# Edge search of a graph layer: one-hots with the chunk outside and rows in a run, and twelve tiles' means and variances by ScalarE

## The chip, the cores and the metric

The kernel runs on one core of a Trainium2 chip. A core has five engines that work side by side and meet at semaphores: TensorE (PE in the profile, with its weight loads shown apart as PEld), VectorE (DVE), ScalarE (ACT), GpSimd (POOL) and SyncE (SP, which here only issues transfers). Each engine works through its own instructions in the order in which they were issued. The metric is the device time of one execution in microseconds, and the time of a kernel is the median of its runs.

## The reference

The kernel computes two layers, each a graph part followed by a mixture of experts, on 3125 nodes with 256 features and 50000 edges. The change concerns only the start of the first graph part. Cut to what matters:

```python
edge_index = jnp.stack([src, dst])
x = x + _L0_gnn_ref(_layernorm(x, axis=-1), edge_index, L0_gnn_W, L0_gnn_b)
x = x + _L0_ffn_ref(_layernorm(x, axis=-1)[None], ...)[0]
x = x + _L1_gnn_ref(_layernorm(x, axis=-1), ..., src, dst)
x = x + _L1_ffn_ref(_layernorm(x, axis=-1)[None], ...)[0]

def _L0_gnn_ref(x, edge_index, W, b):
    dst, src = (edge_index[0], edge_index[1])
    agg = jnp.zeros_like(x).at[dst].set(x[src])
    h = jnp.concatenate((x, agg), axis=-1)
    return h @ W.T + b
```

Here `edge_index[0]`, the array `src` of the inputs, is the node that receives. Each node takes the normalised row of one neighbour: that of the last edge in the list that names it as receiver. The kernel therefore has to find, for every node, the last edge that points to it.

## The kernel before

**Tiling.** The nodes are T = 25 tiles of 128 rows (the last has 53), held in `X`. The 50000 edges are CD = 391 chunks of 128 edges, one edge to each partition. NG = 13 groups of GE = 31 chunks make up the search; GP is 32, one more than GE.

**The search.** Of a receiver's number, `qi` is the place in its tile (0 to 127) and `ri` the tile (0 to 24). For a group `g`, `one_hots(g)` on VectorE makes three things in bf16: `hot`, which holds a one where an edge's place is met (128 values for each of the group's chunks), `tiles[:, 0]`, the same for the tile number (25 values), and `tiles[:, 1]`, that one-hot times a power of two that grows with the chunk (`wb`). In the kernel before the chunk is the innermost index of all three (`[P, P, GP]` and `[P, 2, T, GP]`), and the table that the numbers are compared with, `spread`, is laid out in the same way. TensorE then takes, for every chunk, `hot[:, :, j]` as weights and `tiles[:, :, :, j]` as the 50 moving columns and adds up the group in one bank of PSUM (`sa` for even groups, `sb` for odd ones): the sums hold, for every node, how many edges it receives and, in the exponent, the last chunk of the group that has one. ScalarE copies them to `sums`. After the last group VectorE works out from `sums` the last chunk of every node (`expo`, `key`, `last`, ..., `chunk`). GpSimd gathers that chunk's edges (`er`, from the table `etab`), VectorE picks the edge and its sender (`pick`, `pmax`, `nbr`), and GpSimd gathers the sender's row (`near`, from the table `ztab`).

**What runs beside it.** The loop over the 13 groups also carries the normalisation. `stat(X[:, t, :], mvx, t)` takes a tile's mean and variance on VectorE (`bn_stats`, `bn_aggr`), `root` the root of the variance on ScalarE, `scales` the reciprocal and the shift `minus` on VectorE; `norm_x` normalises a tile on ScalarE (`xn`), `plus_bias` adds the bias to `X` on GpSimd, `turn_x` transposes the normalised tile on TensorE and copies it to `hT` on ScalarE, and `times_w` multiplies it by the weights, copies the product to `zs` on ScalarE and stores it in `ztab`. `edge_rows` writes `etab`, and `gate_products` works on the gates' weights in the first iterations. Transfers of zeros into later tables (`clears`) and of the edges (`wrows`, `wtab`) are issued by SP in the same loop.

**Order.** The order of the instructions on every engine is that of the program (a manual schedule of all five). One iteration `g` issues: `one_hots(g + 2)`, two groups ahead of the matmuls and into one of three buffers; the statistics of tile `g`; at even `g` the scales of the two tiles before; the matmuls of group `g`; `root`; the copy to `sums`; `edge_rows`; then `turn_x` for tile g - 3 and `times_w` for tile g - 4, and at even `g` `norm_x` and `plus_bias` for the tiles g - 2 and g - 1. The remaining twelve tiles have their statistics in the last two iterations (`late`): 13 to 18 at g = 11, and 19 to 24 at g = 12. After the loop come the last two `scales`, the search's end from `expo` on, and `norm_x`, `turn_x` and `times_w` for the remaining tiles.

**Other one-hots in the kernel.** `count_edges` (lines 1212 to 1233) and `list_steps` (lines 794 to 805, with the matmuls of line 788) make one-hots with the chunk outside: the number is held twice side by side, and two helpers lay both operands out in pairs of neighbours:

```python
def pairs(ap, n):
    return ap[:, :, None, :].to_broadcast([P, ap.shape[1], n // 2, 2])
def in_pairs(ap):
    return ap.rearrange("p m (n i) -> p m n i", i=2)
```

Lines that the text names: 376, 378 and 380 (the one-hots), 427 (the search's weights and matmuls), 431 (`sums`), 263 and 264 (`stat`), 267 (`root`), 270 and 271 (`scales`), 274 (`xn`), 312 and 313 (`turn_x`), 320 and 323 (`times_w`), 326 (`ztab`), 338 (`plus_bias`), 449 (`expo`), 502 (`er`), 508 to 515 (picking the edge), 519 (`near`), 1013 (the experts' first matmul), 1489 (a Square with an accumulated sum, in the second layer).

## Time and profile before

| | us |
|---|---|
| median of 3 runs (1099.32 to 1104.02) | 1102.59 |
| the profiled execution | 1105.5 |
| its span, from the first to the last instruction | 1103.7 |
| PE busy in it | 1001.9 (91%) |
| DVE busy | 603.2 (55%) |
| ACT busy | 325.2 (29%) |
| POOL busy | 339.7 (31%) |
| the 391 search matmuls, first and last start | 10.3 and 72.2 |

The busy time of an engine is the time in which at least one of its instructions was under way; a matmul counts until its end, and matmuls overlap, so a busy PE need not be at its peak. The mean granted clock of TensorE was 0.945 of full speed. The search is over in the first 75 us of the span; the experts of the first layer start at about 159 us. In views of the trace, a line gives the start of an instruction or of several alike in us, their length together, the engine, the line of the kernel, what was written from what, the shape and the number; in square brackets stands how long the engine had been idle before, and what ended that.

### The profile page before, as it was taken

The page shows a single profiled execution, that of the slowest core. Times are in us where ns is not written, and L with a number is a line of the kernel's source. Part 1 is how long each engine was busy: PE and PEld are TensorE (multiplying, and loading weights), DVE is VectorE, ACT ScalarE, POOL GpSimd, SP SyncE. Part 2 cuts the span into 40 slices and gives each one's busy share as a digit, 9 for nine tenths or more (in the row PEclk, how much of TensorE's full clock was granted, in tenths as well). Part 3 has the DMA queues.
Part 4 walks back from the last instruction along what each step waited for, and adds up shares of the span by engine and source line. Part 5 has one row for each costly group of instructions (what it writes and reads, how often), then busy time and mean ns, then how long its engine had stood idle before and what let it go on. Part 6 is the DMA issues. An engine that isn't in the chain of part 4 may idle for free. (4 is left out here: it accounts for less than half of the span.)

```text
span 1103.7 us, 16184 instructions
## 1 busy us (share of the span) xinstructions
PE 1001.9 (91%) x6057; PEld 755.0 (68%) x6057; DVE 603.2 (55%) x1571; ACT 325.2 (29%) x712; POOL 339.7 (31%) x357
## 2 busy tenths in 40 slices
PE   6998569998999999999998889999999999998990
PEld 6986436664667667777766668877877878665670
DVE  9975873772645556665544144354157253486563
ACT  1353411221335566666422112121011111312110
POOL 1236445422433112222322111011012235365450
PEclk9979779998999999999999989999989999898995
DMA  7665464532368767776552080411113112764875
GB/s 215 218 174 167 133 215 128 166 128 87 121 207 282 262 229 282 272 253 227 189 174 75 23 330 6 159 81 60 64 57 117 50 48 82 235 216 155 275 260 175
DMA packets 121073, 182.09 MB, mean 165 GB/s; under 512 B 20370, under 2 KB 97143, under 8 KB 120864
## 3 DMA queue, kind: packets, MB, share of 16 engines
q1 hardware_dynamic: 98947, 123.68, 34.7%
q0 software_dynamic: 13200, 34.14, 9.4%
q10 hardware_dynamic: 8836, 23.13, 5.5%
q8 instruction: 50, 0.82, 0.3%
q14 instruction: 40, 0.32, 0.1%
HBM read 108.30 MB, written 74.64 MB: 166 GB/s over the span
## 5 line engine op out<-in xcount | busy, mean ns | idle before, releaser
L1013 PE MATMUL big<-xs,w 128*128 128x512 f32 (+1 forms) x640 | 283.6, 566 | 7.2 <-ACT hid L1017 7.1
L1026 PE MATMUL y<-w,hid 128*128 128x256 f32 x1120 | 270.8, 387 | 6.8 <-DVE y L1031 5.4
L1026 PEld LDWEIGHTS y<-w,hid 128*128 128x128 f32 x1120 | 203.9, 191 | 33.6 <-DVE y L1031 8.1
L1667 PEld LDWEIGHTS <-at 128*128 128x128 bf16 x1875 | 186.7, 100 | 35.7 <-DMA at<-atab 9.2
L1035 POOL DMA_INDIRECT ytab<-y,put x112 | 123.5, 1102 | 206.8 <-DVE y L1031 146.9
L1017 ACT ACTIVATE hid<-big,bt 128x512 f32<-128x512 f32 (+1 forms) x160 | 101.3, 634 | 231.7 <-PE big L1013 208.4
L1013 PEld LDWEIGHTS big<-xs,w 128*128 128x128 f32 x640 | 112.8, 194 | 72.7 <-issue 36.6
L1667 PE MATMUL big<-parts,at 128*128 128x256 bf16 x1200 | 152.9, 282 | 8.2 <-DMA at<-atab 8.2
L1031 DVE TENSOR_TENSOR y<-y,b2t 128x256 f32<-128x256 f32 x112 | 47.2, 423 | 110.1 <-PE y L1026 109.3
L970 POOL DMA_INDIRECT g<-xtab,take x56 | 56.9, 1016 | 154.3 <-PE tr L987 115.9
L1232 PEld LDWEIGHTS <-hq 128*128 128x128 bf16 x800 | 57.2, 98 | 61.0 <-issue 40.4
L1212 DVE TENSOR_TENSOR hq<-qs,iota_b 128x2048 bf16<-128x2048 bf16 x50 | 61.1, 1222 | 54.2 <-PE sb L1232 54.2
L1667 PE MATMUL sa<-parts,at 128*128 128x256 bf16 x525 | 63.6, 273 | 0.0
L988 DVE COPY xs<-tr 128x512 f32<-128x512 f32 (+1 forms) x64 | 37.1, 618 | 48.3 <-PE tr L987 48.3
L1233 ACT CAST at<-sa 128x400 bf16<-128x400 f32 x100 | 49.1, 491 | 47.7 <-PE sa L1232 45.1
L1076 DVE SCALAR_TENSOR_TENSOR X<-y,weight,X 128x256 f32<-128x256 f32 (+1 forms) x78 | 37.7, 506 | 42.4 <-DMA y<-ytab 41.4
L1477 ACT COPY hT<-tr 128x512 f32<-128x512 f32 x25 | 14.4, 586 | 152.5 <-PE tr L1475 152.5
L1233 ACT CAST at<-sb 128x400 bf16<-128x400 f32 x100 | 49.0, 490 | 31.6 <-PE sb L1232 30.1
L1504 POOL TENSOR_TENSOR X<-X,kept 128x256 f32<-128x256 f32 x14 | 10.4, 770 | 129.7 <-DVE kept L496 129.7
L1215 DVE TENSOR_TENSOR hc<-cs,iota_b 128x1600 bf16<-128x1600 bf16 x50 | 49.2, 985 | 0.0
L1469 DVE SCALAR_TENSOR_TENSOR both<-big,deg,feat 128x256 f32<-128x256 f32 x16 | 7.7, 480 | 70.3 <-PE big L1667 70.2
L427 PEld LDWEIGHTS <-hot 128*128 128x128 bf16 x391 | 40.4, 150 | 6.6 <-issue 3.6
(349 smaller groups left out, 1244.0 us busy)
## 6 DMA issues: line engine op xcount, KB each, us to landing
w<-in_fW SPq DMA_DIRECT2D x32, 1024.0 KB
atab<-at ACTq DMA_DIRECT2D x25, 800.0 KB
at<-atab SPq DMA_DIRECT2D x25, 800.0 KB
ytab<-zero_b SPq DMA_DIRECT2D x10, 1024.0 KB
y<-ytab SPq DMA_DIRECT2D x19, 512.0 KB
w<-in_mw SPq DMA_DIRECT2D x32, 256.0 KB
xtab<-zero_b SPq DMA_DIRECT2D x6, 1024.0 KB
rows<-xtab SPq DMA_DIRECT2D x8, 512.0 KB
```

What stands on the lines that cost most here:

```text
L427: nc.tensor.matmul(pg, hot[:, :, j], tiles[:, :, :, j], start=(j == 0), stop=(j == n - 1))
L970: nc.gpsimd.indirect_dma_start(out=g, out_offset=None, in_=tabs[h][0], in_offset=bass.IndirectOffsetOnAxis(ap=routed[h].column(c)[0], axis=0))
L1013: nc.tensor.matmul(ph[:, :n * P], w1[:, i, c * P:(c + 1) * P], turned[k][:, i, :n * P], start=(i == 0), stop=(i == KD - 1))
L1017: nc.scalar.activation(hid[:, c, :n * P], ph[:, :n * P], act, bias=bt[:, 0, c:c + 1])
L1026: nc.tensor.matmul(py, hid[:, c, j * P:(j + 1) * P], w2[:, c, :], start=(c == 0), stop=(c == nh - 1))
L1031: nc.vector.tensor_add(y, py, b2t)
L1035: dma = nc.gpsimd.indirect_dma_start(out=tabs[h][1], out_offset=into, in_=y, in_offset=None, bounds_check=2 * tokens(h) - 1, oob_is_err=False)
L1212: nc.vector.tensor_tensor(in_pairs(hq), pairs(qs[:, mine], P), in_pairs(iota_b[:, None, :].to_broadcast([P, n, P])), OP.is_equal)
L1215: nc.vector.tensor_tensor(in_pairs(hc), pairs(cs[:, mine], C), in_pairs(iota_b[:, None, :C].to_broadcast([P, n, C])), OP.is_equal)
L1232: nc.tensor.matmul(pa[:, j], hq[:, g + j, :], hc[:, g + j, :], start=True, stop=True)
L1233: nc.scalar.copy(at[:, :, W * (g0 + g):W * (g0 + g + 4)].rearrange("p i (g w) -> p i g w", w=W), pa.rearrange("p g i w -> p i g w"))
L1667: nc.tensor.matmul(sums[a][:, t - a, :], at[t][:, i, :], parts[:, i, k, :], start=False, stop=(i == T - 1 and k == 2 and t == b - 1))
```

## The change

The one-hots of the search turn round: `hot` becomes `[P, GE, P]` and `tiles` `[P, GE, 2, TP]`, with TP = 26, so that the values of one chunk lie in a run. The numbers `qb` and `rb` and the powers `wb` are held twice side by side, and the comparisons use `pairs` and `in_pairs`. The table `spread` (128 x 32 values) gives way to `iota_2` (128 values); the padding to GP and the memsets that filled it go.

The statistics of tiles 13 to 24 leave VectorE. In iteration `g` from 0 to 11, `sum_x` has ScalarE add up tile 13 + g (an Identity activation with an accumulated output), and GpSimd scales the sum to the mean and to its negative; one iteration later `square_x` has ScalarE add up the squares of the tile less its mean, and GpSimd scales that to the variance. The roots of tiles 13 to 18 are taken at g = 11, as before; those of tiles 19 to 24 at g = 12, after the copy of the sums and the last square.

```diff
--- before.py
+++ after.py
@@ -23,7 +23,7 @@
 LA = 1
 CD = (E + P - 1) // P
 GE = 31
-GP = GE + 1
+TP = T + T % 2
 NG = (CD + GE - 1) // GE
 BESIDE = 10
 OWN_AT = (2, 3, 4, 6, 7)
@@ -132,8 +132,8 @@
     make_identity(nc, ident)
     lanei = const.tile([P, 1], I32)
     nc.gpsimd.iota(lanei, pattern=[[0, 1]], base=0, channel_multiplier=1 << 12)
-    wexp = const.tile([P, GP], I32)
-    nc.gpsimd.iota(wexp, pattern=[[8, GP]], base=3, channel_multiplier=0)
+    wexp = const.tile([P, GE], I32)
+    nc.gpsimd.iota(wexp, pattern=[[8, GE]], base=3, channel_multiplier=0)
     nodei = const.tile([P, T], I32)
     nc.gpsimd.iota(nodei, pattern=[[P, T]], base=0, channel_multiplier=1)
     rowi = const.tile([P, 2], I32)
@@ -349,35 +349,36 @@
             nc.sync.dma_start(out=wrows[119:, :WR - 1, i, :], in_=edges(119 * WR * B, [[1, 1], [B, WR - 1]]))
             nc.sync.dma_start(out=wrows[119:, WR - 1, i, :], in_=edges(E - P, [[1, 1]]))
         clears = [c for h in range(2) for c in (clear_steps(tabs1[h][1]),)]
-        spread = ep.tile([P, P, GP], BF16, bufs=1)
-        nc.vector.tensor_copy(spread, iota_i[:, :P, None].to_broadcast([P, P, GP]))
-        nc.vector.tensor_scalar(wexp[:, GE:], wexp[:, GE:], 0, None, OP.mult)
+        iota_2 = ep.tile([P, P], BF16, bufs=1)
+        nc.vector.tensor_copy(iota_2, iota_i[:, :P])
+
         nc.vector.tensor_scalar(wexp, wexp, 23, None, OP.logical_shift_left)
-        wb = ep.tile([P, GP], BF16, bufs=1)
-        nc.vector.tensor_copy(wb, wexp.bitcast(F32))
+        wb = ep.tile([P, GE, 2], BF16, bufs=1)
+        nc.vector.tensor_copy(wb, wexp.bitcast(F32)[:, :, None].to_broadcast([P, GE, 2]))
         qi = ep.tile([P, NG * GE], I32, bufs=1)
         nc.vector.memset(qi[:, CD:], 0)
         ri = ep.tile([P, NG * GE], I32, bufs=1)
         nc.vector.memset(ri[:, CD:], -1)
-        qb = ep.tile([P, NG, GP], BF16, bufs=1)
-        nc.vector.memset(qb, 0.0)
-        rb = ep.tile([P, NG, GP], BF16, bufs=1)
-        nc.vector.memset(rb, -1.0)
         nc.vector.tensor_scalar(qi[:, :CD], si_all, P - 1, None, OP.bitwise_and)
         nc.vector.tensor_scalar(ri[:, :CD], si_all, 7, None, OP.arith_shift_right)
-        nc.vector.tensor_copy(qb[:, :, :GE], qi.rearrange("p (g c) -> p g c", c=GE))
-        nc.vector.tensor_copy(rb[:, :, :GE], ri.rearrange("p (g c) -> p g c", c=GE))
+        qb = ep.tile([P, NG * GE, 2], BF16, bufs=1)
+        nc.vector.tensor_copy(qb, qi[:, :, None].to_broadcast([P, NG * GE, 2]))
+        rb = ep.tile([P, NG * GE, 2], BF16, bufs=1)
+        nc.vector.tensor_copy(rb, ri[:, :, None].to_broadcast([P, NG * GE, 2]))
         sums = ep.tile([P, NG, 2, T], F32, bufs=1)
         hots = {}
 
         def one_hots(g):
             if g < NG:
-                hot = ep.tile([P, P, GP], BF16, name="hot", bufs=3)
-                nc.vector.tensor_tensor(hot, qb[:, g, None, :].to_broadcast([P, P, GP]), spread, OP.is_equal)
-                tiles = ep.tile([P, 2, T, GP], BF16, name="tiles", bufs=3)
-                nc.vector.tensor_tensor(tiles[:, 0], rb[:, g, None, :].to_broadcast([P, T, GP]),
-                                        spread[:, :T, :], OP.is_equal)
-                nc.vector.tensor_tensor(tiles[:, 1], tiles[:, 0], wb[:, None, :].to_broadcast([P, T, GP]), OP.mult)
+                a, b = g * GE, (g + 1) * GE
+                hot = ep.tile([P, GE, P], BF16, name="hot", bufs=3)
+                nc.vector.tensor_tensor(in_pairs(hot), pairs(qb[:, a:b], P),
+                                        in_pairs(iota_2[:, None, :].to_broadcast([P, GE, P])), OP.is_equal)
+                tiles = ep.tile([P, GE, 2, TP], BF16, name="tiles", bufs=3)
+                nc.vector.tensor_tensor(in_pairs(tiles[:, :, 0, :]), pairs(rb[:, a:b], TP),
+                                        in_pairs(iota_2[:, None, :TP].to_broadcast([P, GE, TP])), OP.is_equal)
+                nc.vector.tensor_tensor(in_pairs(tiles[:, :, 1, :]), in_pairs(tiles[:, :, 0, :]), pairs(wb, TP),
+                                        OP.mult)
                 hots[g] = hot, tiles
 
 
@@ -393,28 +394,37 @@
             nc.scalar.copy(et[:b - a], pe[:b - a])
             nc.sync.dma_start(out=etab[a:b], in_=et[:b - a])
 
-        def statistics(t):
-            if t < T:
-                stat(X[:, t, :], mvx, t)
+        sumx = ep.tile([P, T, 3], F32, bufs=1)
+
+        def sum_x(t):
+
+            if NG <= t < T:
+                junk = ep.tile([P, D], F32, name="junk", bufs=2)
+                nc.scalar.activation(junk, X[:, t, :], AF.Identity, accum_out=sumx[:, t, 0:1])
+                nc.gpsimd.tensor_scalar(sumx[:, t, 1:2], sumx[:, t, 0:1], -1.0 / D, None, OP.mult)
+                nc.gpsimd.tensor_scalar(mvx[:, t, 0:1], sumx[:, t, 0:1], 1.0 / D, None, OP.mult)
+
+        def square_x(t):
+
+            if NG <= t < T:
+                junk = ep.tile([P, D], F32, name="junk", bufs=2)
+                nc.scalar.activation(junk, X[:, t, :], AF.Square, bias=sumx[:, t, 1:2], accum_out=sumx[:, t, 2:3])
+                nc.gpsimd.tensor_scalar(mvx[:, t, 1:2], sumx[:, t, 2:3], 1.0 / D, None, OP.mult)
 
         one_hots(0)
         constants()
         one_hots(1)
         half = (NG + T) // 2
-        late = {NG - 2: (NG, half), NG - 1: (half, T)}
         lag = NG - BESIDE
         more = gate_products(ep)
         next(more)
         for g in range(NG):
             one_hots(g + 2)
-            statistics(g)
+            stat(X[:, g, :], mvx, g)
             if g % 2 == 0 and g:
                 scales(mvx, g - 2, g)
-            if g >= NG - 2:
-                for t in range(*late[g]):
-                    statistics(t)
-                if g == NG - 1:
-                    scales(mvx, *late[NG - 2])
+            if g == NG - 1:
+                scales(mvx, NG, half)
             if g == 1:
                 lanef = ep.tile([P, 1], F32, bufs=1)
                 nc.vector.tensor_copy(lanef, lanei)
@@ -424,11 +434,15 @@
             n = min(GE, CD - g * GE)
             pg = bank([P, 2, T], F32, "sb" if g % 2 else "sa", 1)
             for j in range(n):
-                nc.tensor.matmul(pg, hot[:, :, j], tiles[:, :, :, j], start=(j == 0), stop=(j == n - 1))
+                nc.tensor.matmul(pg, hot[:, j, :], tiles[:, j, :, :T], start=(j == 0), stop=(j == n - 1))
             root(mvx, g, g + 1)
-            if g >= NG - 2:
-                root(mvx, *late[g])
+            if g == NG - 2:
+                root(mvx, NG, half)
             nc.scalar.copy(sums[:, g], pg)
+            sum_x(NG + g)
+            square_x(NG + g - 1)
+            if g == NG - 1:
+                root(mvx, half, T)
             if 2 <= g < 2 + len(parts_e):
                 edge_rows(*parts_e[g - 2])
             next(more, None)
```

## The prediction

> **What bounds the kernel now.** I first read the span in 20 us stretches, then the groups of the search's tiles, then the timeline around its end. In the stretches the columns are busy us (and instructions) of each engine, granted TensorE clock and DMA:
>
> ```profile
> core 0: us, PE busy (x) PEld busy (x) DVE busy (x) ACT busy (x) POOL busy (x), PEclk, DMA share, GB/s
> 20.00:40.00 20.00, 19.95 (x158) 18.93 (x159) 19.62 (x30) 5.40 (x21) 4.61 (x4) 1.00 0.72 215
> 40.00:60.00 20.00, 20.00 (x155) 18.34 (x154) 19.23 (x28) 7.33 (x24) 4.35 (x5) 0.77 0.60 199
> 60.00:80.00 20.00, 18.99 (x129) 16.11 (x129) 17.04 (x57) 10.87 (x32) 5.41 (x7) 0.80 0.54 141
> ```
>
> The change lies wholly in the first 75 us. There PE and DVE are both full while ACT and POOL have room. So neither a cheaper PE nor a cheaper DVE alone is worth its own saving; the order of the waits decides. The tile view of `hot` (min/median/max ns, first and last start) names the two loads:
>
> ```profile
> L427 PEld LDWEIGHTS <-hot x391: 135/149/309, 9.3 to 72.1; 128*128 128x128 bf16 x196
> L376 DVE TENSOR_TENSOR hot<-qb,spread x13: 2258/2282/2292, 6.9 to 58.6; 128x4096 bf16<-128x4096 bf16 x13
> ```
>
> The timeline lets a search group be compared with two later loops that already hold one-hots in pairs, rows in a run (start, length, what):
>
> ```profile
> 41.08 3.24 PE L427 MATMUL sa<-tiles,hot 128*128 128x50 bf16 x31
> 330.93 0.34 PE L1232 MATMUL sb<-hc,hq 128*128 128x100 bf16 x4
> 147.32 0.39 DVE L798 TENSOR_TENSOR col<-cb,iota_b 128x448 bf16<-128x448 bf16 x1
> 147.74 0.39 DVE L803 TENSOR_TENSOR col<-col,tile 128x448 bf16<-128x448 bf16 x1
> 148.56 0.57 PE L788 MATMUL sa<-col,lane 128*128 128x64 bf16 x14 [1.53 <-DVE col L805]
> ```
>
> A search matmul costs (3.24-0.28)/30 = 0.099 us from one to the next, or 0.104 us over the group; the run form costs (0.57-0.19)/13 = 0.029 us with 64 columns and (0.34-0.21)/3 = 0.045 with 100 (0.19 and 0.21 are the mean lengths of one in the groups by shape). The end of the loop, DVE, PE and ACT together:
>
> ```profile
> 58.63 2.29 DVE L376 TENSOR_TENSOR hot<-qb,spread 128x4096 bf16<-128x4096 bf16 x1 [0.37 <-PE sb L427]
> 61.44 0.58 DVE L380 TENSOR_TENSOR tiles<-tiles,wb 128x800 bf16<-128x800 bf16 x1
> 62.67 0.16 DVE L271 SCALAR_TENSOR_TENSOR minus<-mvx 128x2 f32<-128x2 f32 x1
> 65.74 1.10 ACT L274 ACTIVATE xn<-X,minus,mvx 128x256 f32<-128x256 f32 x2
> 68.29 0.62 PE L312 MATMUL tr<-ident,xn 128*128 128x128 f32 x2
> 70.47 2.05 PE L427 MATMUL sa<-tiles,hot 128*128 128x50 bf16 x19
> 72.55 0.20 ACT L431 COPY sums<-sa 128x50 f32<-128x50 f32 x1 [1.07 <-PE sa L427]
> 72.79 0.49 DVE L449 TENSOR_SCALAR expo<-sums 128x325 int32<-128x325 int32 x1 [0.81 <-ACT sums L431]
> 73.99 1.58 ACT L274 ACTIVATE xn<-X,minus,mvx 128x256 f32<-128x256 f32 x3
> ```
>
> The reader is to see: DVE makes one-hots almost without a wait (0.37 us in all) until 62.0; PE runs 8 us behind (the last group's matmuls start at 70.47); two outputs leave the loop, the sums at 72.79 (the search's end, then the gathers of `er`) and ACT's normalising at 73.99 (then `ztab`). They meet where the first `near` is gathered, and from there to the first expert matmul at 158.97 PE waits again and again, so the rest follows them:
>
> ```profile
> 95.54 0.95 POOL L502 DMA_INDIRECT er<-etab,chunk  x1 [0.30 <-DVE nbr L515]
> 97.68 0.95 POOL L519 DMA_INDIRECT near<-ztab,nbr  x1 [1.19 <-issue]
> ```
>
> **What the Trainium skill says.** "SBUF — State Buffer", section "Door 1: The DMA port swizzle (why `[64,N]` ≈ `[32,N]`)", says that SBUF has lines of 16 bytes and that each access to a new line pays a penalty; the trace agrees: weights read 64 bytes apart load in 149 ns, those in a run (line L1232) in 98. "VectorE: DVE Perf Modes", section "The perf-mode tier table (the rule you actually need)", gives a bf16 tensor_tensor of 2048 elements 1224 ns; L1212, in pairs, takes 1222. "ScalarE: Activation LUTs", section "What ACT_TABLE_LOAD costs", adds about 93 ns for each per-partition pointer operand; the trace agrees: 603 ns for `xn` with two, 417 for the Square of line L1489 with none. "GPSIMD Engine Reference", section "1. Specifications", says that POOL shares its SBUF interfaces with VectorE; the trace agrees: L378 takes 0.57 us, and 1.09 beside the POOL add of L338.
>
> **The change, part by part.**
>
> Matmuls: 391 at 0.03 instead of 0.104 take about 29 us from PE. This is not the gain: the PE then waits for DVE. A group of 31 falls from 3.2 to 1.1 us.
>
> One-hots on DVE: from 2048 to 4096 elements the time grows by 1.06 us, 0.516 ns each, so `hot` with 3968 saves 0.066 us, 12 times before the last: 0.8. `tiles` goes from 800 to 806: nothing. The output rows now lie apart; L798 and L803 write such rows at the same packed rate (448 elements, 0.39), so I add nothing for it.
>
> Start: the `spread` cast of 2.28 us fell into the wait for POOL's `wexp` (ends 4.07), so nothing is won. L354 (0.19) and two memsets (0.59 from start to start) go. The casts of `qb` and `rb` double to 806 elements: at the packed rate of `spread` they stay at 0.57, at one element a cycle they become 0.98, so together 0 to 0.84 more. Whether `si_all` has landed 0.8 us sooner isn't shown. The first one-hot moves by between -0.8 and +0.1; I take -0.3.
>
> Statistics: twelve bn_stats and bn_aggr leave DVE, about 0.53 us each, 6.4 in all. They lie after the last one-hot, where DVE would otherwise wait for the last matmuls: worth nothing by themselves, but without them the later gain couldn't be had.
>
> ACT: twelve sums (0.42 from start to start, read of the accumulator included) and twelve squares (0.51, one pointer more), 11 us. In a group of 4.3 us ACT then uses about 2.8 (even groups: root 0.2, sums 0.08, these two 0.93, hT 0.27, zs 0.28, two xn 1.02), so DVE covers it; at the end it isn't covered (below). There are no more table loads in the instruction order than before.
>
> POOL: 36 instructions on 128x1, not in this trace; the nearest are iotas and memsets of that width at 0.10 to 0.13, so 4.7 us. A square waits for POOL's minus-mean of the group before; ahead of it on POOL are the two adds of L338, which end some 2 us before. So no stall on ACT. Through the shared port they cost DVE between 0 (none meets a two-input instruction) and 4 us; I take 0.5. The DMA queue of SP issues the same in the same order; only the waits on ACT move.
>
> **The sum.** D, the last `hot`'s start, is 58.63-0.37 (no wait for PE) -0.8-0.3+0.5 = 57.7. From D: scales end 4.0 later (62.74-58.63, less 0.07); on ACT root, sums, sum, square, hT and zs of that iteration take xn(8) to D+5.7; its transposition ends D+6.7, times_w D+7.8 (1.06 at full clock), the last 19 matmuls D+8.7. ACT meanwhile does xn(9), two roots, sums, sum, square, hT, zs, root, and copies the last sums at D+8.8. New here: the last square (to D+9.5), POOL's variance (0.2 with the hand-over), the root of the last six (0.3), and DVE's reciprocal and minus (0.35), all ahead of `expo`: D+10.4 = 68.1, against 72.79: -4.7. The first xn after the loop: D+10.6 = 68.3, against 73.99: -5.7. The gather of `er` would then end at 96.5-4.7 and `ztab` be there at 97.7-5.7, both at 92; the `near` gathers wait on the first, and so does DVE's own picking: **-4.6 us**. The profiled execution (1105.5, span 1103.7) becomes 1100.9; the median of the three runs lies 2.9 lower, at 1102.6, and becomes **1098.0**.
>
> A change of 0.5% is 5.5 us, about what a measurement of this kernel can tell from no change; the forecast lies just within it.
>
> **Rivals.**
>
> More comes through (faster): casts packed and `si_all` early (another 0.5), no port losses (0.5), and full clock from 92 to 120 where the before ran at half for some stretches (1 to 2). For it: PE has 29 us less to do in a stage where it was full. Against: DVE's one-hots cost what they did. 7 us less: 1095.6; 1092.5 if each of them is had in full and `expo` follows the last one-hot still sooner.
>
> The tail eats it (same): if the clock is at half for the tail (as it was from 66 to 70), the transposition, times_w and the last matmuls take some 1.7 longer, and ACT's 0.9 per group is not covered in a group or two: -1 to -2.5, 1100 to 1101.5.
>
> ACT waits for POOL (slower): were the minus-mean stuck behind the two L338 adds (2.2 us when DVE contends), the in-order ACT would stop with root, hT and xn behind it, and DVE's scales would wait for the root. 2 us in each of six even groups is 12 us: 1102.6-4.6+12 = 1110. It decides from 4.6 us, 0.8 per even group; slower by over 0.5% from 1.7. Against it: one whole group lies between the POOL instruction and its use. DVE stalled 0.3 us by each of the 36 POOL instructions would give the same sign.
>
> That the change doesn't do what it says: its matmuls might keep their distance, being set by the issue and not by the reading; then DVE's relief of the tail alone stays, some 2 us. L788 speaks against it.
>
> **How the numbers follow.** The forecast case, -2.5 to -5.5, has 0.43; more than that 0.37; -2.5 to +5.5 (tail, no faster matmuls, or a wait just covered) 0.11; slower by over 5.5 0.09. So faster 0.37, same 0.54, slower 0.09. The forecast's own range is 1097 to 1100; the one given reaches to 1092.5 for the faster case and to 1104.0 for the tail case and part of the ACT wait, and leaves out some 2 in 10.
>
> **What would show it.** Right: the 31 matmuls of a group in about 1.1 us, their weights at 98 ns; `hot` at 2.22; `expo` near 68 with DVE waiting for ACT's root ahead of it; the first `near` near 93; later stages shifted alike. Wrong: `hot` or `tiles` above 2.3 and 0.6 in groups without L338; ACT waiting for POOL in the loop; DVE's `hot` waiting for PE; or a shift at `near` that is gone at the first expert matmul.

## The result, and the profile after

The changed kernel takes 1094.42 us (median of 10 runs, 1087.80 to 1097.86) against 1100.33 (10 runs, 1098.17 to 1106.32) for the kernel before; three of these ten are the runs of the table above. The ratio formed from the single runs is 0.9931, 95% interval 0.9903 to 0.9959; of 1102.6 us that is 7.6 us less, 4.5 to 10.7. The two medians alone differ by 5.9 us. The forecast of 4.6 lies at the small end. Its profiled execution has a span of 1088.5 us and took 1090.33.

The first view is again the span in 20 us stretches:

```profile
core 0: us, PE busy (x) PEld busy (x) DVE busy (x) ACT busy (x) POOL busy (x), PEclk, DMA share, GB/s
20.00:40.00 20.00, 14.83 (x176) 12.69 (x173) 19.59 (x33) 9.62 (x42) 14.73 (x18) 1.00 0.70 205
40.00:60.00 20.00, 12.13 (x185) 9.84 (x184) 19.62 (x28) 10.60 (x42) 17.09 (x20) 0.91 0.69 230
60.00:80.00 20.00, 16.20 (x90) 12.87 (x91) 9.40 (x32) 18.07 (x56) 11.66 (x19) 0.91 0.72 196
```

PE, which had been full between 40 and 60 us, now idles for 40% of it; DVE is as full as before and is the only bound left. ACT is busy 4.2 and 3.3 us longer in the first two stretches. POOL shows 14.73 and 17.09 us where it had 4.61 and 4.35, which is far more than 36 tiny instructions should come to. The tile view of `hot` and one group in the timeline:

```profile
L437 PEld LDWEIGHTS <-hot x391: 95/118/291, 8.9 to 65.6; 128*128 128x128 bf16 x196
L375 DVE TENSOR_TENSOR hot<-qb,iota x13: 2193/2216/2219, 6.6 to 55.9; 128x3968 bf16<-128x3968 bf16 x13
50.59 0.96 PE L437 MATMUL sb<-tiles,hot 128*128 128x50 bf16 x31
```

31 matmuls take 0.96 us in this group, instead of 3.24. Five of the twelve groups of 31 are as short; the first five take 1.45 to 1.50, and the mean of the twelve is 1.22. One `hot` takes 2.216 us instead of 2.282, and the last `hot` starts at 55.95 instead of 58.63. The end of the loop in the timeline:

```profile
55.95 2.20 DVE L375 TENSOR_TENSOR hot<-qb,iota 128x3968 bf16<-128x3968 bf16 x1
...
62.10 1.10 ACT L274 ACTIVATE xn<-X,minus,mvx 128x256 f32<-128x256 f32 x2
62.76 0.58 PE L312 MATMUL tr<-ident,xn 128*128 128x128 f32 x2 [3.15 <-ACT xn L274]
63.14 1.97 PE L320 MATMUL y<-gWn,hT 128*128 128x264 f32 x4
64.90 1.00 PE L437 MATMUL sa<-tiles,hot 128*128 128x50 bf16 x19
65.94 0.20 ACT L441 COPY sums<-sa 128x50 f32<-128x50 f32 x1 [0.22 <-PE sa L437]
66.72 0.21 POOL L412 TENSOR_SCALAR mvx<-sumx 128x1 f32<-128x1 f32 x1 [1.86 <-ACT junk L411]
66.96 0.30 ACT L267 ACTIVATE dev<-mvx,eps 128x6 f32<-128x6 f32 x1 [0.32 <-POOL mvx L412]
67.29 0.19 DVE L270 RECIPROCAL mvx<-dev 128x6 f32<-128x6 f32 x1 [1.19 <-ACT dev L267]
67.60 0.48 DVE L463 TENSOR_SCALAR expo<-sums 128x325 int32<-128x325 int32 x1
67.69 1.59 ACT L274 ACTIVATE xn<-X,minus,mvx 128x256 f32<-128x256 f32 x3
```

After the last group the four new steps can be read in order: ACT's sums (65.94), POOL's variance (66.72), ACT's root (66.96), DVE's reciprocal (67.29), and only then `expo` at 67.60, 5.2 us earlier than before, and the first `xn` at 67.69, 6.3 earlier. Further on in the timeline:

```profile
72.80 1.19 POOL L516 DMA_INDIRECT er<-etab,chunk  x1 [1.20 <-DVE has L480]
...
91.47 0.94 POOL L533 DMA_INDIRECT near<-ztab,nbr  x1 [1.22 <-issue]
```

The first `near` gather is 6.2 us earlier (97.68), the first addition of a neighbour to `X` 8.0 (108.9 to 100.9), and the first expert matmul 7.8 (158.97 to 151.20). That is as much as the ratio gives. The profiled executions differ by 15.2 us; from there on the shift stays between 6.5 and 8.3 us until 750 us, and the rest arises behind that, where nothing of the change runs. Single runs of the changed kernel spread over 10 us, and nothing in the runs ties that rest to the change.

### The profile page after: what moved, and what is told of

Its sections match the earlier page's. It is cut to its first block, busy times and chain, and to the rows that moved or that the text cites. A ratio compares the mean times of both kernels' runs of the same rounds, so it can differ in the third digit from the quotient of the medians.

```text
span 1088.5 us, 16243 instructions
## 1 busy us (share of the span) xinstructions
PE 969.7 (89%) x6057; PEld 723.8 (66%) x6057; DVE 592.4 (54%) x1544; ACT 334.2 (31%) x760; POOL 361.0 (33%) x393
## 5 line engine op out<-in xcount | busy, mean ns | idle before, releaser
L1040 PEld LDWEIGHTS y<-w,hid 128*128 128x128 f32 x1120 | 203.9, 191 | 34.5 <-DVE y L1045 9.0
L1681 PEld LDWEIGHTS <-at 128*128 128x128 bf16 x1875 | 183.5, 99 | 32.6 <-DMA at<-atab 8.9
L1049 POOL DMA_INDIRECT ytab<-y,put x112 | 122.9, 1097 | 208.1 <-DVE y L1045 144.6
L1031 ACT ACTIVATE hid<-big,bt 128x512 f32<-128x512 f32 (+1 forms) x160 | 101.3, 634 | 232.3 <-PE big L1027 208.9
L1681 PE MATMUL big<-parts,at 128*128 128x256 bf16 x1200 | 146.7, 275 | 8.0 <-DMA at<-atab 8.0
L1246 PEld LDWEIGHTS <-hq 128*128 128x128 bf16 x800 | 57.2, 98 | 61.0 <-issue 40.3
L1247 ACT CAST at<-sb 128x400 bf16<-128x400 f32 x100 | 49.0, 490 | 31.7 <-PE sb L1246 30.3
L1518 POOL TENSOR_TENSOR X<-X,kept 128x256 f32<-128x256 f32 x14 | 10.4, 773 | 127.2 <-DVE kept L510 127.2
L1654 POOL DMA_INDIRECT xtab<-kept,place x28 | 27.5, 982 | 47.2 <-DVE place L1651 21.9
```

Of the source, the lines that this page charges most:

```text
L1031: nc.scalar.activation(hid[:, c, :n * P], ph[:, :n * P], act, bias=bt[:, 0, c:c + 1])
L1040: nc.tensor.matmul(py, hid[:, c, j * P:(j + 1) * P], w2[:, c, :], start=(c == 0), stop=(c == nh - 1))
L1049: dma = nc.gpsimd.indirect_dma_start(out=tabs[h][1], out_offset=into, in_=y, in_offset=None, bounds_check=2 * tokens(h) - 1, oob_is_err=False)
L1246: nc.tensor.matmul(pa[:, j], hq[:, g + j, :], hc[:, g + j, :], start=True, stop=True)
L1247: nc.scalar.copy(at[:, :, W * (g0 + g):W * (g0 + g + 4)].rearrange("p i (g w) -> p i g w", w=W), pa.rearrange("p g i w -> p i g w"))
L1681: nc.tensor.matmul(sums[a][:, t - a, :], at[t][:, i, :], parts[:, i, k, :], start=False, stop=(i == T - 1 and k == 2 and t == b - 1))
```

## The experiments

Runs that share a group shared a chip. In three groups the kernel before takes 1173.31 to 1180.80 us; in the group of the result above and in that of the last experiment it takes 1100.33 and 1099.35. These are called the longer and the shorter chip below. What sets the length is not known: the record has the number 14 for the chip of one longer group and for that of the last, shorter one. So each ratio is to the kernel before of its own group, and starts in us are compared within one length; even there the kernel before differs by 7.5 us from group to group. "CK" is the changed kernel. Each expectation numbers its own theories. Starts are in us, of one profiled execution each; the group of 31 is one of the shortest of its run:

| kernel | group of 31 | last `hot` | `expo` | first `er` | first `near` | first expert matmul | ratio to before |
|---|---|---|---|---|---|---|---|
| before, longer chip | 3.24 | 60.6 | 74.8 | 82.2 | 113.0 | 189.1 | 1 |
| statistics alone | 3.26 | 59.3 | 75.3 | 81.2 | 112.1 | 185.8 | 1.0013 [0.9997, 1.0030] |
| layout alone | 0.97 | 57.8 | 70.3 | 75.6 | 105.0 | 180.2 | 0.9989 [0.9976, 1.0003] |
| `hot` alone in runs | 2.86 | 55.8 | 67.2 | 72.4 | 102.4 | 177.5 | one run, 1169.69 us |
| `tiles` alone in runs | 2.05 | 57.2 | 69.4 | 75.1 | 104.5 | 181.1 | one run, 1168.48 us |
| CK, longer chip | 0.96 | 55.8 | 66.8 | 72.2 | 102.5 | 178.0 | 0.9933 [0.9906, 0.9960] |
| no small POOL work | 0.96 | 56.0 | 66.2 | 71.6 | 103.3 | 179.3 | 0.9944 [0.9921, 0.9967] |
| early statistics | 0.96 | 57.3 | 64.9 | 70.4 | 101.1 | 176.4 | 0.9936 [0.9913, 0.9959] |
| `expo` held back | 0.96 | 55.6 | 71.5 | 76.6 | 99.8 | 175.7 | 0.9894 [0.9870, 0.9918] |
| eight `zs` | 0.96 | 55.8 | 66.7 | 71.9 | 101.3 | 175.3 | 0.9925 [0.9897, 0.9953] |
| early statistics, eight `zs` | 0.96 | 57.1 | 65.3 | 71.4 | 103.0 | 179.0 | 0.9921 [0.9893, 0.9949] |
| before, shorter chip | 3.24 | 58.6 | 72.8 | 78.8 | 97.7 | 159.0 | 1 |
| CK, shorter chip | 0.96 | 55.9 | 67.6 | 72.8 | 91.5 | 151.2 | 0.9931 [0.9903, 0.9959] |
| `er` held back, shorter chip | 0.96 | 55.8 | 66.7 | 80.7 | 98.5 | 158.6 | 1.0054 [1.0037, 1.0072] |

### The statistics alone

The changed kernel with the one-hots of the kernel before.

```diff
-hot = ep.tile([P, GE, P], BF16, name="hot", bufs=3)
+hot = ep.tile([P, P, GP], BF16, name="hot", bufs=3)
...
-tiles = ep.tile([P, GE, 2, TP], BF16, name="tiles", bufs=3)
+tiles = ep.tile([P, 2, T, GP], BF16, name="tiles", bufs=3)
...
-nc.tensor.matmul(pg, hot[:, j, :], tiles[:, j, :, :T], start=(j == 0), stop=(j == n - 1))
+nc.tensor.matmul(pg, hot[:, :, j], tiles[:, :, :, j], start=(j == 0), stop=(j == n - 1))
```

> The kernel after, with the one-hots and matmuls of the kernel before (chunk inside, strided reads); only the twelve tiles' statistics by ScalarE and GpSimd are kept. Theory 1 (DVE's one-hots pace the loop, PE's backlog sets its end): a search matmul stays at 0.104 us, PE stays 7 to 8 us behind the one-hots, and the last square, POOL's variance and the root now lie behind the last sums: expo at 73 to 75 us (72.8 before), first expert matmul at 159 to 161, time 0 to 2 us above before. Theory 2 (the relief of DVE is the gain): expo near 68, 5 to 7 us below before. Theory 3 (the matmuls alone are the gain): as before within 1 us.

Measured: 1174.32 us, ratio 1.0013 (0.9997 to 1.0030), as good as nothing. A group and the end of the loop in its timeline:

```profile
46.78 3.28 PE L436 MATMUL sb<-tiles,hot 128*128 128x50 bf16 x31
...
71.55 2.07 PE L436 MATMUL sa<-tiles,hot 128*128 128x50 bf16 x19
...
74.67 0.30 ACT L267 ACTIVATE dev<-mvx,eps 128x6 f32<-128x6 f32 x1 [0.32 <-POOL mvx L411]
...
75.32 0.49 DVE L462 TENSOR_SCALAR expo<-sums 128x325 int32<-128x325 int32 x1
```

PE still comes to the last group only at 71.55. DVE, which no longer has statistics to take, waits for it, and the ring of ACT, POOL, ACT and DVE is then added behind. So relieving DVE alone doesn't bring `expo` forward.

### The layout alone

The kernel before with the new one-hots; the twelve tiles' statistics stay on DVE.

```diff
-nc.tensor.matmul(pg, hot[:, :, j], tiles[:, :, :, j], start=(j == 0), stop=(j == n - 1))
+nc.tensor.matmul(pg, hot[:, j, :], tiles[:, j, :, :T], start=(j == 0), stop=(j == n - 1))
```

> The kernel before with the one-hots and matmuls of the kernel after; the twelve tiles' statistics stay on VectorE in the last two iterations. Theory 1: PE's backlog goes, the last one-hot starts near 56 us as in after, then fourteen statistics and the scales (about 8.5 us) stand between it and expo on DVE: expo at 68.5 to 69.5, the first normalising after the loop (line 274) at about 69.5, 3 to 4 us below before and 2 to 3 above after. Theory 2: no gain, expo at 72 or later. Theory 3: the whole gain, as after within 1 us.

Measured: 1171.50 us, ratio 0.9989 (0.9976 to 1.0003). The same places in its timeline:

```profile
46.84 0.96 PE L428 MATMUL sa<-tiles,hot 128*128 128x50 bf16 x31
...
69.60 0.30 ACT L267 ACTIVATE dev<-mvx,eps 128x6 f32<-128x6 f32 x1 [2.83 <-DVE mvx L264]
...
69.81 0.18 ACT L432 COPY sums<-sa 128x50 f32<-128x50 f32 x1
...
70.33 0.49 DVE L450 TENSOR_SCALAR expo<-sums 128x325 int32<-128x325 int32 x1
```

The groups are as short as in CK, and the very last matmul starts at 65.1. But ACT now stands in a root that waits 2.83 us for DVE's statistics (69.60), with the copy of the last sums queued behind it. What PE gave up, DVE's statistics took: `expo` starts at 70.3, between the 75.3 of the other half and the 66.8 of both. In the profiles three quarters of the way from the statistics alone to CK is made at `near` (105.0, between 112.1 and 102.5), but of the 5.6 us by which the first expert matmul comes earlier than with the statistics alone, only 2.8 stand in the medians of the same group (1174.32 and 1171.50). The expectation of 3 to 4 us was too high.

The two halves give +1.5 and -1.3 us, and both together -7.9 in a later group (0.67% of 1178.7). But the kernels before of these two groups differ by 5.4 us themselves, CK was not run in the first, and in absolute time the layout alone (1171.50) is next to CK (1171.05). Inside the first group only the two kernels of the next section come near CK; their single runs are 1.8 and 3.0 us below the layout alone. So how much of the time is a surplus of both halves isn't shown. That `expo` follows the later of two chains, PE's groups or DVE's statistics, is what the two timelines show.

### Which operand's rows cost the matmul its time

Two kernels, each with one of the two one-hots in runs and the other strided as before. First `hot` (the weights) in runs, `tiles` (the moving columns) strided:

```diff
-nc.tensor.matmul(pg, hot[:, j, :], tiles[:, j, :, :T], start=(j == 0), stop=(j == n - 1))
+nc.tensor.matmul(pg, hot[:, j, :], tiles[:, :, :, j], start=(j == 0), stop=(j == n - 1))
```

> The kernel after with hot in runs but tiles as before (chunk inside, moving columns 64 bytes apart). If the distance of the search's matmuls is set by reading the weights: weight loads at 98 ns and 31 matmuls in 1.0 to 1.2 us, as in after. If it is set by reading the moving columns: 31 in about 3.2 us. If both count: in between, about 2.

Then the other way round:

```diff
-nc.tensor.matmul(pg, hot[:, j, :], tiles[:, j, :, :T], start=(j == 0), stop=(j == n - 1))
+nc.tensor.matmul(pg, hot[:, :, j], tiles[:, j, :, :T], start=(j == 0), stop=(j == n - 1))
```

> The kernel after with tiles in runs but hot as before (chunk inside, weights 64 bytes apart). If the weights set the distance: weight loads at 149 ns and 31 matmuls in about 3.2 us. If the moving columns do: 1.0 to 1.2 us. If both: about 2.

Tile view and timeline, first of `hot` in runs, then of `tiles` in runs:

```profile
L439 PEld LDWEIGHTS <-hot x391: 97/115/291, 8.0 to 65.2; 128*128 128x128 bf16 x196
48.25 2.86 PE L439 MATMUL sa<-tiles,hot 128*128 128x50 bf16 x31
```

```profile
L440 PEld LDWEIGHTS <-hot x391: 137/168/309, 9.3 to 67.4; 128*128 128x128 bf16 x196
43.08 2.04 PE L440 MATMUL sb<-tiles,hot 128*128 128x50 bf16 x31
```

From one matmul to the next (the group less the length of one, over 30): both strided 0.099 us, moving columns strided 0.087 ((2.86 - 0.25)/30), weights strided 0.062 ((2.04 - 0.19)/30), both in runs 0.026 ((0.96 - 0.19)/30). The two strides don't add, they hide each other: repairing the weights alone is worth 12 ns, the moving columns alone 37, both 73.

The start of `expo` says something else. With `hot` in runs and groups still of 2.86 us, it lies at 67.2, next to CK's 66.8, though PE is full (first number behind the 20.00; the clock, PEclk, is third from the end):

```profile
40.00:60.00 20.00, 20.00 (x191) 18.49 (x191) 18.98 (x29) 9.88 (x38) 16.25 (x20) 1.00 0.61 203
```

A group, a transposition and a `times_w` take PE 3.8 us there (groups start at 48.25, 52.06, 55.86 and 59.67), less than the 4.2 us that DVE takes for an iteration in CK, so PE catches up. In the kernel before they take 4.6 to 5.3 us in the same place. Only 0.4 of that is the group: the kernel before was granted half the clock for part of it (0.77 on average), which this run was not, and its `times_w` took up to 1.97 us in place of 1.05. CK had half the clock at its end (0.72 from 62 to 68 us, here 1.00). So PE's whole iteration has to be set against DVE's, and how much of this run's early `expo` is due to the clock is open.

`tiles` alone in runs, with the shorter group, is later (69.4): its `hot` is the larger one again, the last starts at 57.2, and the last 19 matmuls take 1.34 us. Its one run is still the shorter of the two, 1168.48 us against 1169.69; single runs of one kernel spread by more than that.

### The changed kernel again, without POOL's small operations, and with early statistics

CK itself for comparison:

> The changed kernel once more, beside the other versions of this group, so that they share one chip with it. Theory 1 (the stretch of the edge search ends 5 to 6 us earlier and nearly all of it is handed on to the end): 4 to 9 us under the kernel before, a ratio of 0.993 to 0.996. Theory 2 (the transfers to and from ztab, not expo, set when the gate's first loop can run): on a chip with slower transfers the gain shrinks to 0 to 3 us, a ratio of 0.997 to 1.000. In both, expo starts between 67 and 68.5 us and the last hot near 56.

Measured: 1171.05 us, ratio 0.9933 (0.9906 to 0.9960), the same as in the result above.

In the second, squares are taken without the mean, and DVE forms mean and variance of six tiles with three small instructions, twice:

```diff
-nc.gpsimd.tensor_scalar(sumx[:, t, 1:2], sumx[:, t, 0:1], -1.0 / D, None, OP.mult)
-nc.gpsimd.tensor_scalar(mvx[:, t, 0:1], sumx[:, t, 0:1], 1.0 / D, None, OP.mult)
...
-nc.scalar.activation(junk, X[:, t, :], AF.Square, bias=sumx[:, t, 1:2], accum_out=sumx[:, t, 2:3])
-nc.gpsimd.tensor_scalar(mvx[:, t, 1:2], sumx[:, t, 2:3], 1.0 / D, None, OP.mult)
+nc.scalar.activation(junk, X[:, t, :], AF.Square, accum_out=sumx[:, t, 2:3])
```

> The changed kernel without any of GpSimd's small operations in the loop (squares without the mean taken off, the means and variances of six tiles at a time formed by three small VectorE operations). It asks what the 35 small GpSimd operations, which took 0.2 to 1.9 us each, cost the others. Theory 1 (they only wait beside VectorE's two-input operations and cost nothing): last hot starts 0.3 us earlier to 0.5 us later than in the changed kernel, expo 0 to 0.6 us earlier, the run within 1.5 us. Theory 2 (the port that VectorE and GpSimd share takes time from VectorE): last hot over 1 us earlier, expo 1.5 us earlier or more, the run 1.5 to 3 us shorter.

Measured: 1172.63 us, ratio 0.9944 (0.9921 to 0.9967). Groups of POOL in the first 66 us (busy us and mean ns of one behind the bar, then idle time before them), first of CK, then of the kernel without the small operations:

```profile
L338 POOL TENSOR_TENSOR X<-X,gbt 128x256 f32<-128x256 f32 x10 | 16.2, 1638 | 0.8 <-ACT xn L274 0.8
L404 POOL TENSOR_SCALAR sumx<-sumx 128x1 f32<-128x1 f32 x12 | 12.4, 1033 | 25.0 <-ACT junk L403 25.0
L405 POOL TENSOR_SCALAR mvx<-sumx 128x1 f32<-128x1 f32 x12 | 4.0, 335 | 0.0
```

```profile
L338 POOL TENSOR_TENSOR X<-X,gbt 128x256 f32<-128x256 f32 x10 | 9.4, 962 | 50.9 <-ACT xn L274 50.9
```

The first instruction on 128x1 of a pair takes POOL 1.03 us on average, the second 0.34, and the addition of `gbt` goes from 0.96 to 1.64 beside them. Yet the last `hot` starts at 55.8 and 56.0: ahead of it DVE loses nothing that can be seen. Behind it, it does lose. CK's additions of `gbt` come later and still run beside the last `tiles`, whose first instruction takes 1.10 us (at 57.95) in place of 0.57 here (at 58.17), and `expo` starts 0.7 us later than here. The time of the run shows nothing of it (theory 1 of the expectation).

The third takes all sums and squares in the first eight groups and forms moments and roots for twelve tiles well ahead of the end:

```diff
+early = {0: (13,), 1: (14, 15), 2: (16,), 3: (17, 18), 4: (19,), 5: (20, 21), 6: (22,), 7: (23, 24)}
...
-            sum_x(NG + g)
-            square_x(NG + g - 1)
-            if g == NG - 1:
-                root(mvx, half, T)
+            for t in early.get(g, ()):
+                sum_x(t)
+                square_x(t)
```

> The changed kernel with the sums of its twelve tiles spread over the first eight groups (one tile in an even group, two in an odd one), squares without the mean taken off, means and variances formed for all twelve at once by VectorE, and their roots and scales two to four groups before the end; GpSimd's small operations are gone and nothing of the statistics is left behind the last matmul group. Theory 1 (the tail's ring of junk, GpSimd, root, reciprocal is what follows the last group): expo about 2 us earlier than in the changed kernel, at 65 to 66 us, and the run 1 to 3 us shorter. Theory 2 (the last matmul group at half clock and times_w ahead of it hold expo, the statistics end beside them): expo within 0.7 us of the changed kernel's, the run within 1 us.

Measured: 1172.68 us, ratio 0.9936 (0.9913 to 0.9959). In its timeline `expo` follows the copy of the last sums at once:

```profile
64.53 0.20 ACT L446 COPY sums<-sa 128x50 f32<-128x50 f32 x1
...
64.92 0.48 DVE L466 TENSOR_SCALAR expo<-sums 128x325 int32<-128x325 int32 x1
```

From the copy to `expo` it is 0.39 us here. So taking the ring away from behind the last group was worth 1.9 us at `expo`, 1.4 at `near` and 1.6 at the first expert matmul, as its theory 1 had it, though the last `hot` starts 1.4 us later; the time of the run doesn't show it (1.6 us longer by the medians, within both intervals).

### `expo` held back

Two more comparisons of the size of `hot`, with no reader, ahead of `expo` on DVE:

```diff
 scales(mvx, half, T)
+for _ in range(2):
+    late = ep.tile([P, GE, P], BF16, name="hot", bufs=3)
+    nc.vector.tensor_tensor(in_pairs(late), pairs(qb[:, :GE], P),
+                            in_pairs(iota_2[:, None, :].to_broadcast([P, GE, P])), OP.is_equal)
```

> The changed kernel with two further comparisons of the size of hot (about 2.2 us each, results unused) on VectorE just ahead of expo, behind the last scales: expo 4.4 us later, normalisation of X by ScalarE as before. Theory 1 (what is gained at expo reaches the end one for one): first er gather, first near gather and first expert matmul each 4 to 4.5 us later, the run 4 to 5 us longer, a ratio to the changed kernel of 1.004. Theory 2 (X and ztab, whose work does not go through expo, set the start of the gate's first loop): first er gather later by 4.4 us, first expert matmul by less than 2 us, the run by less than 2 us.

Measured: 1167.35 us, ratio 0.9894 (0.9870 to 0.9918), 3.7 us shorter than CK in the same group. Neither theory had a gain. `er` begins 4.4 us later and `near` 2.7 us earlier. CK's timeline, then that of this kernel:

```profile
72.20 1.19 POOL L516 DMA_INDIRECT er<-etab,chunk  x1 [0.98 <-DVE has L480]
...
91.54 0.38 ACT L323 COPY zs<-y 128x264 f32<-128x264 f32 x1 [6.02 <-remote]
...
98.92 1.27 SPq L326 DMA_DIRECT2D ztab<-zs  x2
102.51 1.10 POOL L533 DMA_INDIRECT near<-ztab,nbr  x1 [12.84 <-issue]
```

```profile
76.57 1.19 POOL L520 DMA_INDIRECT er<-etab,chunk  x1 [2.79 <-DVE has L484]
...
97.08 0.34 SPq L326 DMA_DIRECT2D ztab<-zs  x1
...
99.77 0.95 POOL L537 DMA_INDIRECT near<-ztab,nbr  x1 [5.68 <-issue]
```

On this chip POOL has issued its fourteen `er` gathers at 89.7 and then waits 12.84 us for `near`: it isn't the search that holds the gather of `near` here. In CK ACT stands still for 6.02 us up to 91.54, inside the work for `ztab`, in a wait that the profile puts down to "remote" and no more; the last `ztab` store is issued at 99.9 (97.1 in the kernel with `expo` held back).

What `near` waits for is that store. In all eleven profiles of the longer chip the first `near` starts 2.6 to 3.2 us behind its issue; on the shorter chip it is 3.5 us in the kernel before, 3.7 in CK and 10.0 with `er` held back. And in ten of the eleven `near` starts 34.5 to 36.2 us behind the first `xn` after the loop, with `expo` held back 32.4. So on the longer chip the change works through the normalising: that `xn` starts at 77.07 us before and at 67.51 in CK, and `near` at 113.0 and 102.5.

### The kernel before on the longer chip, and eight buffers for `zs`

> The kernel before once more, for its profile on the chip that the other runs of this group use. Theory 1 (its edge search ends as on the first chip, and the later stretch is what differs): last hot at 58 to 59.5 us, expo at 72.5 to 74 us. If the chip is the one with the longer times (some 1170 to 1180 us), first near at 109 to 112 us, 7 to 9 us behind the changed kernel's 102.5, with ScalarE waiting for buffers of zs in between as it does there. Theory 2 (the changed kernel's order brings the wait for zs about): before has no such wait and its first near comes at 103 to 106 us.

Measured in its one run: first `er` 82.2, first `near` 113.0, with a wait of ACT there too (4.63 us ahead of a `zs` copy at 97.26, again put down to "remote"). So the gap of 30.9 us between `er` and `near` (30.3 in CK) belongs to the longer chip and not to the change; on the shorter chip it is 18.9 before and 18.7 after.

> The changed kernel with eight buffers of zs in place of four, so that ScalarE and TensorE can run on while stores to ztab are under way. It asks why two further comparisons ahead of expo made the run 3.7 us shorter, not longer. Theory 3 (on this chip the last stretch before the first near gather is held by ScalarE waiting for a zs buffer, since the er gathers slow the stores; later gathers collide less): last zs at 86 to 92 us in place of 99.5, first near 4 to 10 us earlier than in the changed kernel, the run 3 to 8 us shorter. Theory 4 (the stores themselves are late, whatever the buffers): last zs early, but first near within 1.5 us of the changed kernel's, the run within 2 us. On a chip where ScalarE does not wait for zs, nothing moves (within 1.5 us) under either.

```diff
-                turning["z"] = pool.tile([P, 2, D + NE], F32, name="zs", bufs=4)
+                turning["z"] = pool.tile([P, 2, D + NE], F32, name="zs", bufs=8)
```

Measured: 1171.28 us, ratio 0.9925 (0.9897 to 0.9953). ACT's wait is still there (5.32 us ahead of a `zs` copy at 89.09) and `near` comes at 101.3. A lack of `zs` buffers isn't the reason.

> The changed kernel with both the early statistics (sums of the twelve tiles in the first eight groups, moments on VectorE, no small GpSimd operations) and eight buffers of zs. Theory 3 (zs buffers hold the stretch up, and behind them the tail of the statistics): 1 to 3 us under the version with eight buffers alone, expo at 65 us. Theory 4 (the stores are late whatever the buffers): no shorter than the version with early statistics alone, a ratio to the kernel before of 0.993 to 0.995.

Measured: 1171.08 us, ratio 0.9921 (0.9893 to 0.9949), `expo` at 65.3, `near` at 103.0. Theory 3 falls with the run before; the early statistics again bring `expo` forward and nothing that the time shows.

### `er` held back without more work on DVE

If the later gathers of `er` had made the gain, another way to hold them back should bring it too. GpSimd adds the bias to seven more tiles ahead of them, and VectorE has seven additions less later:

```diff
-            if t <= HALVES[0][1]:
+            if t <= HALVES[0][1] + 7:
                 plus_bias(nc.gpsimd, t - 1)
...
-                for t in range(n, T):
+                for t in range(n + 7, T):
                     plus_bias(nc.vector, t)
```

> The changed kernel with the bias of seven more tiles (14 to 20) added to X by GpSimd behind their normalisation, in place of VectorE later; GpSimd issues the er gathers behind these, so that they begin at about 76.5 us as in the version with two further comparisons, but expo stays at 67 us and VectorE does nothing more. If this chip is the one with the longer times: Theory 5 (the two comparisons shortened the run because the er gathers came later and met the ztab stores less): last zs 2 to 4 us earlier than in the changed kernel, first near at 98 to 101 us, a ratio to the kernel before of 0.988 to 0.991. Theory 6 (it was something else in them, or chance in how ScalarE's stop near 80 to 92 us falls): first near at 102 to 106 us, a ratio of 0.992 to 0.996. On a chip without that stop: first near 3 to 4.5 us later than in the changed kernel, at 95 to 96 us, a ratio of 0.995 to 0.998.

The group fell on the shorter chip: 1105.80 us against 1099.35, ratio 1.0054 (1.0037 to 1.0072). The delay was also larger than meant, 7.9 us in place of 4. POOL's timeline:

```profile
80.74 1.19 POOL L516 DMA_INDIRECT er<-etab,chunk  x1 [0.20 <-issue]
...
97.28 0.95 POOL L516 DMA_INDIRECT er<-etab,chunk  x1 [0.30 <-DVE extra L550]
98.53 0.95 POOL L533 DMA_INDIRECT near<-ztab,nbr  x1 [0.30 <-issue]
```

Here `near` follows the fourteenth `er` with no wait, 14 steps of about 1.25 us after the first. `er` is 7.9 us later than in CK, `near` 7.1, the first expert matmul 7.4: on this chip a microsecond at the search's end is carried on nearly whole. The run lost more than that, some 13.6 us (1.0054 over 0.9931), and where the other 6 come from is open. What shortened the run with `expo` held back is open too: a second way to delay `er` was never measured on the longer chip.

On the shorter chip only CK and the version with `er` held back were run. The one with `expo` held back is shorter than CK on the longer chip, and was not run on the other.

## Why the prediction was right, and where it was short

The sign and the mechanism held. The likeliest case, 4.6 us, lies at the small end of the measured interval (4.5 to 10.7), and the 7.6 us, like the 5.9 between the medians, belong to the case "more comes through", which had 0.37 against the 0.43 of the forecast case. The median of 1094.42 lies in the range given, and below the 1097 to 1100 of that case. By the prediction's steps:

- **Matmuls.** 1.1 us for a group was forecast, 1.22 measured on average: 0.96 at best, and 1.45 to 1.50 in the first five, up to 32 us; just behind them a matmul of `times_w`, too, takes 0.65 us, and 0.39 from 38 us on. The thirteen groups take 25.5 us less than before, where 29 were forecast. That the time of a group is not the gain itself agrees with `hot` alone in runs, 2.86 us a group and `expo` nearly as early as in CK; but that run had the full clock throughout.
- **Statistics "worth nothing by themselves, but without them the later gain couldn't be had".** The two timelines show it: with the statistics alone DVE waits for PE's last group, with the layout alone the statistics hold `expo` 3.5 us behind CK's. The times, +1.5 us and -1.3, fit this, as far as one group without CK can show it.
- **One-hots on DVE.** `hot` 2.216 us (2.22 forecast), `tiles` 0.57 and 0.60 in the middle: rows that lie apart are written at the packed rate.
- **Start.** First `hot` 0.33 us earlier (0.3 forecast), by another account: the casts of `qb` and `rb` took the dear end (0.98 us each), and POOL's `wexp` came 2 us sooner since `spread` was gone; DVE then waited 1.64 us for `si_all`.
- **POOL and the port.** This term was mis-sized twice over. The nearest rows gave 0.10 to 0.13 us for an instruction on 128x1; it takes 0.2 to 1.9. And DVE was charged 0.5 us ahead of D, where it gains instead: there the two instructions on `tiles` take 15.07 us from start to start for twelve groups, against 15.95 before, as three of them fall beside an addition of `gbt` and no longer six. DVE pays behind D. The additions, which the small operations delay, run into the last `tiles`; two lines of CK, then that of the kernel before:

```profile
55.03 3.69 POOL L338 TENSOR_TENSOR X<-X,gbt 128x256 f32<-128x256 f32 x2
...
58.07 1.10 DVE L378 TENSOR_TENSOR tiles<-rb,iota 128x806 bf16<-128x806 bf16 x1
```

```profile
60.84 0.57 DVE L378 TENSOR_TENSOR tiles<-rb,spread 128x800 bf16<-128x800 bf16 x1
```

- **D, the last `hot`'s start.** 57.7 forecast, 55.95 measured. The port explains 1.4 of the 1.75 (0.5 charged, 0.9 gained); the rest is spread over small steps.
- **The tail.** D + 10.4 forecast, D + 11.65 measured. About half of the 1.25 is that `tiles`: the scales end at D + 4.65 in place of 4.0. The other half is the rival "the tail eats it": `times_w` at 63.14 takes 1.97 us in place of 1.06 (granted clock 0.50 from 64 to 66), and the last 19 matmuls end at D + 9.95 in place of 8.7. The ring behind the copy of the last sums takes 1.66 us, priced at about 1.6. That the two errors, D 1.75 us too late and the tail 1.25 too short, nearly cancel and leave `expo` at 67.60 against 68.1 is luck.
- **From `expo` to `near`.** -4.6 forecast, -6.2 measured, with 18.7 us from the first `er` to the first `near` as before (18.9). The forecast had `ztab` and the gathers ready together, by taking the start of `near` for the arrival of `ztab`. The last store was issued at 94.16 before and at 87.77 now; with the 2.65 us that most of the longer chip's profiles show behind it, an estimate, `ztab` was ready about 1 us before `near` started. `er` itself gained 6.0, 0.8 more than `expo`: its wait now ends with `has` (72.42), and before it ended with `deg`, the instruction behind (77.94 to 78.68).
- **From `near` to the first expert matmul.** No change forecast, -1.6 measured (-1.8 by the first addition of a neighbour): 24 matmuls of `plus_own` took 7.51 us before (from 100.6, with a granted clock of 0.57 between 102 and 106) and 5.76 after (from 94.4, at full clock). This is the "full clock from 92 to 120, 1 to 2 us" that stood in the faster case, and it should have stood in the sum.

ACT waited for POOL nowhere in the loop but for 0.32 us ahead of the last root, so the slower rival never came near its 0.8 us per even group. The forecast's chain from `expo` through `er` to `near` is shown on the shorter chip. On the longer one the same gain appears (0.9933), but there `er` isn't what `near` waits for: it comes through the `ztab` side, whose first `xn` is 9.6 us earlier and whose last store is 10.5 us earlier (one profile each).

## What to carry to other kernels

Where two engines are full side by side, look for the second chain before pricing the first: each half of this change moved the time by less than 2 us, and only both brought `expo` to 67. Lay both operands of a matmul in runs, or don't expect the whole of it from one of them, but ask first whether TensorE, with all its work of an iteration and at the clock it is granted, or the engine that feeds it sets the pace. And when an output is brought forward by microseconds, follow it to the place where its reader really waits, since that can be a different transfer from one group of runs to another.

## What was not expected of the hardware

- A strided moving operand cost more than strided weights: 37 ns saved per matmul by mending the moving columns alone, 12 by the weights alone, 73 by both (0.099 to 0.026 us from one matmul to the next).
- A small POOL operation is held up by DVE and hardly holds it up. On 128x1 it took 0.2 to 1.9 us beside DVE's two-input comparisons, while `hot` kept its 2.2 us. An addition on 128x256 does hold DVE up: `tiles` takes 1.10 us beside it in place of 0.57. The Trainium skill's page "GPSIMD Engine Reference", section "1. Specifications", says that the two share their SBUF interfaces; these runs agree.
- In the kernel before, building the identity took POOL 2.27 us beside the cast of `spread`, and 0.29 after, with the cast gone.
- The cast of `qb` made 806 values, each held twice, in 0.98 us, where the cast of `spread` made 4096 in 2.28 us. The pairs aren't shown to be the reason: the cast of 403 values without them took 0.56 us before.
- More work on DVE made the program 3.7 us shorter in one group on the longer chip. What is shown is a shorter stop of ACT and `ztab` written 2.8 us sooner; why isn't settled.
